# Expert outputs of a decoder layer: gathered and summed at the end, or scattered with accumulation as each tile is done

## The chip, the cores and the metric

The kernel runs on one core of a Trainium2 chip. The metric is the device time of one execution in microseconds (us): the median of several runs. The core has five engines that work beside each other and meet at semaphores: PE (matrix products), DVE (vector operations), ACT (activations and copies), POOL (general, and the issue of indirect DMAs) and SP (issue of DMAs). ACT and POOL issue DMAs too. Each engine does its instructions in order.

## What is computed

x is 4 sequences of 1024 tokens of 256 numbers. The reference is a decoder layer of three blocks:

```python
# after a gated delta-rule attention block on x (L0_attn) and its layernorm:
x = _layernorm(x + _L0_xattn_ref(x, ctx_1024, _lenS2, ...), axis=-1)
x = _layernorm(x + _L0_ffn_ref(x, router_w, gate_w, gate_b, up_w, up_b, down_w, down_b), axis=-1)

# _L0_ffn_ref: 8 experts, each token uses 2
probs = jax.nn.softmax(xf @ router_w.T, axis=-1)
topv, topi = jax.lax.top_k(probs, TOP_K)
mask = jnp.zeros_like(probs).at[jnp.arange(n)[:, None], topi].set(1.0)
probs = probs * mask
probs = probs / (probs.sum(axis=-1, keepdims=True) + 1e-09)
g = jnp.einsum('nd,edf->nef', xf, gate_w) + gate_b
u = jnp.einsum('nd,edf->nef', xf, up_w) + up_b
h = jax.nn.silu(g) * u
expert_out = jnp.einsum('nef,efd->ned', h, down_w) + down_b
y = jnp.einsum('ne,ned->nd', probs, expert_out)
```

The change is in the last block, in what leads to it, and in a few lines at the kernel's start.

## The kernel before

All numbers are 32-bit. P is 128, B is 4 sequences, D is 256, NE is 8 experts, FF is 512. Tokens are worked on in NS = 8 slabs of 4 x 128.

The first half (project, prepare, scan and their helpers) is the delta-rule attention. It leaves its normalized result in the DRAM tensor xd. At the start of the program, lines 141 to 155 make the DRAM tensors xg and yg, turn the gate and up biases with one transpose into br, store them as rows in bd (L149, on SP) and fill the end of xg with zeros (L153, on ACT).

The cross-attention is a software pipeline over 64 units (slab, sequence, half of the heads): five stages with fixed distances (L1165), interleaved with the generator route of the slab before. Slabs are in SBUF tiles xs with three buffers (slab_in). Route computes a slab's softmax over the experts, its two best experts as one-hot rows sel, their shares, and for both a row of xg: expert e owns a stretch of STRIDE rows, and counts in free say how far it is filled. Then POOL scatters the slab's rows twice, 8 indirect DMAs of 128 rows each (L1145). Shares and rows of all slabs are kept in share and at. For slabs 0 to 4 the slab is stored back to xd and its buffer loads slab i + 3.

When the last unit is done, the memory of the attention is released; SP loads the down weights wdn (L1179), and copies gate, up and down biases to all partitions of ball by two broadcasting DMAs (L1184 and L1188: 4 MB and 1 MB written). ACT reads eight numbers into registers one after another and writes 128 rows of zeros behind each expert's last row (L1264). The function tiles computes from the counts which expert and which rows of xg each of the NT = 71 tiles of 128 rows has (ei, ri), and, with gap and moved, where each token's two results will lie in yg (found).

The loop over tiles (L1337) has five steps at fixed distances: fetch (a DMA of 128 rows of xg into mx, four buffers, three tiles ahead; the first four from ACT, the rest from SP), turned (two transposes and a copy to mxT), hidden (gate and up products against the expert's weights, addressed by a register; DVE adds the biases as sge and pup, ACT does silu, DVE multiplies to mh), turn_h (four transposes and a copy to mhT) and down (the product pdn, DVE adds the bias as my, SP stores 128 rows of yg).

At the end, combine goes over the 8 slabs: for each of 4 sequences and 2 experts POOL gathers 128 rows of yg into part (L1352), DVE multiplies by the share and adds to the slab (L1358), then come mean and variance (L1362, L1363), square root on ACT (L1366), reciprocal and offset on DVE, normalization on ACT (L1370, four per slab) and the store. Slabs 5 to 7 are still in SBUF, the others are loaded again from xd.

Instructions are not in the order of the text: a scheduler puts each engine's instructions in order when the program is built, keeps the dependences, and gives each DMA one of eight semaphores per kind, so that an issue also waits for the earlier DMA of its semaphore.

## Time and profile before

| what | value |
|---|---|
| time, median of 3 runs | 1990.59 us (1987.02 to 1990.92) |
| profiled execution | 1989.58 us |
| its span on the core | 1987.8 us |
| PE busy | 1640.0 us, 83% |
| DVE busy | 1119.5 us, 56% |
| ACT busy | 918.3 us, 46% |
| POOL busy | 549.5 us, 28% |
| DMA moved | 98.97 MB, mean 50 GB/s |

The span is what the instructions of the profiled execution cover; its own time, as measured, is 1.8 us more. Busy times are sums over the whole span, and the stages have different limits, so they are read by stage. A name such as "pdn<-wdn,mhT" is the tile written and the tiles read; L1326 is a line of the kernel before; PEclk is the share of full speed that PE's clock was granted. Each 128-row fp32 product shows as two PE records. "Chain of waits" is the chain of work that ended last, followed back from the end.

### The profile page before, as it was taken

Reading aid. Unit: us, or ns where it says so; the run is one execution under the profiler, and the core shown is the slowest. Engines: PE = TensorE matmul, PEld = TensorE weight load, DVE = VectorE, ACT = ScalarE, POOL = GpSimd, SP = SyncE. Lnnn points to the kernel's source line nnn. Section 1 sums busy time; section 2 is a strip of 40 time slices with the busy share of each in tenths; the row PEclk is TensorE's granted clock in tenths of the full one; section 3 lists DMA queues with packets and bytes.
Section 4 is the critical chain, followed back from the end, with each engine's and each line's share of the span. In section 5 each row is a group of like instructions: output and inputs, shape, how many; then the busy total and the mean of one; then the engine's idle time right before and its main releaser. Section 6 shows DMA issues by size and latency. Waiting matters only on the chain.

```text
span 1987.8 us, 27920 instructions
## 1 busy us (share of the span) xinstructions
PE 1640.0 (83%) x9524; PEld 1163.7 (59%) x9524; DVE 1119.5 (56%) x3199; ACT 918.3 (46%) x2161; POOL 549.5 (28%) x503
## 2 busy tenths in 40 slices
PE   4678898979898888878899999999739999999900
PEld 2456575747575666744676777767616666666600
DVE  4748584857576767434466666566534444444444
ACT  3435463636464545332687776766412222222212
POOL 2222222131222222132345545555410000000065
PEclk9879898989898999789999999999869999999955
DMA  3011010110101011030401100100162111111144
GB/s 113 17 32 23 20 35 17 28 27 22 32 22 33 22 22 44 17 113 0 169 12 33 42 23 32 43 33 22 33 239 77 46 46 46 48 43 48 32 147 136
DMA packets 118347, 98.97 MB, mean 50 GB/s; under 512 B 57803, under 2 KB 106303, under 8 KB 117951
## 3 DMA queue, kind: packets, MB, share of 16 engines
q1 hardware_dynamic: 107135, 75.66, 13.0%
q0 software_dynamic: 6144, 16.79, 2.7%
q10 hardware_dynamic: 4928, 4.74, 0.7%
q8 instruction: 78, 1.28, 0.3%
q14 instruction: 62, 0.51, 0.1%
HBM read 62.12 MB, written 35.03 MB: 49 GB/s over the span
## 4 chain that ended last, share of the span: by engine, by line
PE 49%; DVE 22%; ACT 11%; POOL 8%; issue 5%; DMA 5%; SPq 0%; ACTq 0%; POOLq 0%; DVEq 0%
PE pgt L1299 6%; PE pup L1299 6%; PE pdn L1326 6%; ACT sc L1006 4%; PE pp L257 3%; DMA part<-yg,found 2%; DVE kq L269 2%; DVE v L269 2%; PE pe L432 2%; PE pxo L1040 2%; PE pss L365 2%; DVE bp L455 2%; DVE ut L494 2%; PE pmh L1317 2%; POOL xg L1145 2%
## 5 line engine op out<-in xcount | busy, mean ns | idle before, releaser
L1006 ACT ACTIVATE sc<-sc,ntop,rq 128x77 f32<-128x77 f32 x512 | 182.2, 440 | 71.0 <-DVE ntop L1004 48.2
L1352 POOL DMA_INDIRECT part<-yg,found x64 | 61.3, 958 | 454.7 <-issue 443.7
L1040 PE MATMUL pxo<-vo,aT 128*128 128x256 f32 (+1 forms) x640 | 168.4, 396 | 3.7 <-ACT aT L1025 2.8
L1308 ACT ACTIVATE sge<-sge 128x512 f32<-128x512 f32 x71 | 44.7, 630 | 247.8 <-DVE sge L1307 247.8
L257 PE MATMUL pp<-nT,wqkv 128*128 128x262 f32 x512 | 143.3, 413 | 0.0
L1299 PE MATMUL pgt<-wall,mxT 128*128 x284 | 135.5, 600 | 1.8 <-ACT mxT L1288 1.8
L1299 PE MATMUL pup<-wall,mxT 128*128 x284 | 134.8, 597 | 0.0
L1326 PE MATMUL pdn<-wdn,mhT 128*128 x568 | 134.2, 379 | 0.0
L1040 PEld LDWEIGHTS pxo<-vo,aT 128*128 128x128 f32 (+1 forms) x640 | 117.9, 199 | 21.5 <-ACT aT L1025 5.8
L963 POOL TENSOR_TENSOR rq<-rq,nhalf 128x8 f32<-128x8 f32 x64 | 106.0, 1656 | 76.1 <-DVE rq L962 73.5
L949 PE MATMUL pq<-xwq,xT 128*128 128x512 f32 x256 | 123.0, 603 | 0.5 <-ACT xT L943 0.5
L1011 POOL TENSOR_TENSOR sc<-sc,den 128x616 f32<-128x616 f32 x64 | 77.9, 1218 | 160.7 <-DVE den L1010 77.6
L269 DVE SCALAR_TENSOR_TENSOR v<-pp,cols,v 128x256 f32<-128x256 f32 x192 | 91.3, 476 | 43.9 <-ACT v L267 42.0
L269 DVE SCALAR_TENSOR_TENSOR kq<-pp,cols,kq 128x256 f32<-128x256 f32 x192 | 90.5, 478 | 45.3 <-ACT kq L267 42.8
L257 PEld LDWEIGHTS pp<-nT,wqkv 128*128 128x128 f32 x512 | 96.1, 201 | 33.2 <-issue 16.8
L989 PE MATMUL psc<-kbd,qT 128*128 128x154 f32 x512 | 93.0, 305 | 27.1 <-DVE sc L996 21.9
L1307 DVE TENSOR_TENSOR sge<-pgt,ball 128x512 f32<-128x512 f32 x71 | 49.1, 692 | 112.9 <-PE pgt L1299 112.9
L1326 PEld LDWEIGHTS pdn<-wdn,mhT 128*128 128x128 f32 x568 | 102.5, 190 | 11.0
L685 POOL TENSOR_TENSOR so<-so,nhalf 128x4 f32<-128x4 f32 x32 | 32.4, 1011 | 276.0 <-DVE so L684 276.0
L989 PEld LDWEIGHTS psc<-kbd,qT 128*128 128x128 f32 x512 | 74.6, 196 | 43.3 <-DVE sc L996 30.1
L1299 PEld LDWEIGHTS pup<-wall,mxT 128*128 128x128 f32 x284 | 54.6, 192 | 69.0 <-issue 69.0
L455 DVE SCALAR_TENSOR_TENSOR bp<-pk,nb,ee 128x256 f32<-128x256 f32 x128 | 51.7, 476 | 69.9 <-PE pk L444 40.0
(285 smaller groups left out, 3700.8 us busy)
## 6 DMA issues: line engine op xcount, KB each, us to landing
yg<-my SPq DMA_DIRECT2D x71, 128.0 KB, 1.7
mx<-xg SPq DMA_DIRECT2D x67, 128.0 KB, 2.0
xs<-xd SPq DMA_DIRECT2D x13, 512.0 KB, 4.5
xi<-in_x SPq DMA_DIRECT2D x8, 512.0 KB, 4.1
am<-ab SPq DMA_DIRECT2D x16, 256.0 KB, 4.0
xd<-kd SPq DMA_DIRECT2D x32, 128.0 KB, 2.4
wall<-in_L_ffn_gate_w SPq DMA_DIRECT2D x8, 512.0 KB, 10.5
wall<-in_L_ffn_up_w SPq DMA_DIRECT2D x8, 512.0 KB, 10.8
```

What stands on the lines that cost most here:

```text
L257: mm(pp[:, 0 : 2 * (HALO + P)], lhsT=wqkv[:, kc, c * P : (c + 1) * P], rhs=nT[:, kc, 2 * j : 2 * j + 2, :].rearrange("p b t -> p (b t)"), ...
L269: nc.vector.scalar_tensor_tensor(ch, pre[:, :, n : n + P], cols[:, w0 + n : w0 + n + 1], ch, ALU.mult, ALU.add)
L455: nc.vector.scalar_tensor_tensor(bp[:, :, b * H + h], pk[:, r * 2 * P : (r + 1) * 2 * P].rearrange("p (n t) -> p n t", n=2), made["nb"][:, ...
L949: mm(pq, lhsT=t["xT"][:, kc, :], rhs=xwq[:, kc, c0 : c0 + HH * XD], start=kc == 0, stop=kc == KC - 1,)
L963: nc.gpsimd.tensor_tensor(rq, rq, nhalf[:, :HH], ALU.pow)
L989: mm(ps[:, c * 2 * SC : (c + 1) * 2 * SC], lhsT=qT[:, 2 * g + c, :], rhs=kbd[:, half * XC // 2 + 2 * g + c, b, :], start=True, stop=True,)
L1006: nc.scalar.activation(sc[:, h], sc[:, h], AF.Exp, scale=rq[:, h : h + 1], bias=ntop[:, h : h + 1])
L1011: nc.gpsimd.tensor_tensor(sc, sc, bc(den.unsqueeze(2), [P, HH, SC]), ALU.mult)
L1040: mm(px[:, 0:D], lhsT=aT[:w, c, :], rhs=vo[:w, b, half * NV + c, :], start=half == 0 and c == 0, stop=half == 1 and c == NV - 1,)
L1299: mm(ps, lhsT=t["xT"][:, c, :], rhs=wall[:, bass.ds(e * EW + off + c * FF, FF)], start=c == 0, stop=c == KC - 1,)
L1326: mm(px[:, 0:D], lhsT=t["hT"][:, f, :], rhs=wdn[:, bass.ds(e * EV + f * D, D)], start=f == 0, stop=f == FC - 1,)
L1352: nc.gpsimd.indirect_dma_start(out=g, out_offset=None, in_=yg, in_offset=bass.IndirectOffsetOnAxis(ap=found[:, i, b, k : k + 1], axis=0),)
```

## The change

- The row of a token in xg becomes DX = 260 numbers wide: behind its 256 values are the token's own row number in xd, the number of its first expert, and its two shares. Route writes these four columns into the slab tile xs (now 260 wide) before the scatter; share and at are no longer kept for all slabs, and found, gap and moved are gone. The zero rows behind the experts carry row numbers of 128 spare rows of xd.
- In down, four small DVE operations work out the weight of each row of the tile (mw: the first share where the tile's expert is the row's first expert, else the second) and its row number (mrow). ACT multiplies y by the weight, and POOL adds y to the rows of xd with an indirect DMA that accumulates. yg is gone. mx, mw and mrow have eight buffers, my four, mxT four. Fetch goes four tiles ahead and turned two.
- All eight slabs are stored back to xd after routing. combine loads every slab (five buffers), has no gathers, and the fourth of a slab's normalizations is done on POOL.
- ball is filled by PE: each bias row is copied to all partitions by a product with a column of the identity repeated 128 times, four rows to a PSUM bank, 20 banks, each copied to ball by ACT. The DRAM copy bd and both broadcasts are gone; the down biases come in as 16 rows (brd) at the start.
- The eight registers for the zero rows are loaded in one batch.

In the changed program's order, the banks' products are spread around pr and pcount of the last slab on PE, ACT does twelve of the 20 copies ahead of the load of the eight registers and the others between the zero fills, and each accumulating scatter on POOL waits for the one before. In the attention the engines' order is that of before but for a few places.

The core of the diff (not shown: the new constants, 0:D in place of whole slabs, and tex kept in another pool):

```diff
@@ -138,26 +142,28 @@
-    xg = tc.dram_tile([NROW, D], F32, name="xg")
-    yg = tc.dram_tile([NT * P, D], F32, name="yg")
-
-    bd = tc.dram_tile([2 * NE * FC, P], F32, name="bd")
+    xg = tc.dram_tile([NROW, DX], F32, name="xg")
+
     pbr = bank("pbr")
     nc.tensor.transpose(pbr[0 : 2 * NE * FC, 0:P], cols[:, C_GB:NCOLS], ident)
     br = const.tile([2 * NE * FC, P], F32, name="br")
     nc.vector.tensor_copy(br, pbr[0 : 2 * NE * FC, 0:P])
-    nc.sync.dma_start(out=bd, in_=br)
-    zero = const.tile([P, 1, D], F32, name="zero")
+    brd = const.tile([NE * KC, P], F32, name="brd")
+    nc.scalar.dma_start(out=brd, in_=a["L0_ffn_down_b"].rearrange("e (c n) -> (e c) n", n=P))
+
+    zero = const.tile([P, 1, DX], F32, name="zero")
     nc.gpsimd.memset(zero, 0.0)
+    nc.vector.tensor_scalar_add(zero[:, 0, D : D + 1], nw[:, N_PART : N_PART + 1], float(NS * B * P))
     nc.scalar.dma_start(
-        out=xg[NE * STRIDE :, :].rearrange("(p r) d -> p r d", p=P), in_=bc(zero, [P, NE, D])
+        out=xg[NE * STRIDE :, :].rearrange("(r p) d -> p r d", p=P), in_=bc(zero, [P, NE, DX])
     )
     ab = tc.dram_tile([2 * NQ * B * H, Q * Q], F32, name="ab")
     ub = tc.dram_tile([2 * NQ * B * H, Q * Q], F32, name="ub")
-    xd = tc.dram_tile([NS * B * P, D], F32, name="xd")
+    xd = tc.dram_tile([NS * B * P + P, D], F32, name="xd")
+    nc.scalar.dma_start(out=xd[NS * B * P :, :], in_=zero[:, 0, 0:D])
@@ -1046,13 +1052,11 @@
         if half == 1:
-            x = slabs[i][:, b, :]
+            x = slabs[i][:, b, 0:D]
             nc.vector.tensor_tensor(x, x, px[:, 0:D], ALU.add)
             layernorm(xp, x, x, "c")
-    slots, found = (ek.tile([P, NS, B, 2], I32, name=n) for n in ("slots", "found"))
-    at = ek.tile([P, NS, B, 2], F32, name="at")
-    share = ek.tile([P, NS, B, 2], F32, name="share")
+    slots = ek.tile([P, NS, B, 2], I32, name="slots")
@@ -1122,11 +1126,19 @@
         nc.vector.tensor_tensor(got, pair, bc(pw.unsqueeze(2), [P, B, 2, NE]), ALU.mult)
-        nc.vector.tensor_reduce(share[:, i], got, AX.X, ALU.add)
-        nc.vector.tensor_reduce(red, share[:, i], AX.X, ALU.add)
+        share = rp.tile([P, B, 2], F32, tag="share", name="share")
+        nc.vector.tensor_reduce(share, got, AX.X, ALU.add)
+        nc.vector.tensor_reduce(red, share, AX.X, ALU.add)
         nc.vector.tensor_scalar_add(red, red, 1e-9)
         nc.vector.reciprocal(red, red)
-        nc.vector.tensor_tensor(share[:, i], share[:, i], bc(red.unsqueeze(2), [P, B, 2]), ALU.mult)
+        nc.vector.tensor_tensor(xs[:, :, D + 2 :], share, bc(red.unsqueeze(2), [P, B, 2]), ALU.mult)
+        nc.vector.tensor_scalar(
+            xs[:, :, D], nw[:, N_STEP : N_STEP + B], nw[:, N_PART : N_PART + 1], float(i * B * P), ALU.add, ALU.add
+        )
+        first = rp.tile([P, B, NE], F32, tag="first", name="first")
+        number = nw[:, N_NUM : N_NUM + NE].unsqueeze(1)
+        nc.vector.tensor_tensor(first, sel[:, 0], bc(number, [P, B, NE]), ALU.mult)
+        nc.vector.tensor_reduce(xs[:, :, D + 1], first, AX.X, ALU.add)
         yield
@@ -1137,8 +1149,9 @@
         nc.vector.tensor_tensor(got, pair, bc(place.unsqueeze(2), [P, B, 2, NE]), ALU.mult)
-        nc.vector.tensor_reduce(at[:, i], got, AX.X, ALU.add)
-        nc.vector.tensor_copy(slots[:, i], at[:, i])
+        at = rp.tile([P, B, 2], F32, tag="at", name="at")
+        nc.vector.tensor_reduce(at, got, AX.X, ALU.add)
+        nc.vector.tensor_copy(slots[:, i], at)
         for b in range(B):
@@ -1149,8 +1162,8 @@
                 apart(ins, "scatter")
+        nc.sync.dma_start(out=tokens(i), in_=xs[:, :, 0:D])
         if i + 3 < NS:
-            nc.sync.dma_start(out=tokens(i), in_=xs)
             slabs.append(slab_in(sp, i + 3))
@@ -1181,16 +1194,21 @@
     ball = bl.tile([P, B_D + NE * D], F32, name="ball")
-    nc.sync.dma_start(
-        out=ball[:, 0:B_D].rearrange("p (n c) -> p n c", c=P),
-        in_=bc(bd.rearrange("(o n) c -> o n c", o=1), [P, 2 * NE * FC, P]),
-    )
-    nc.sync.dma_start(
-        out=ball[:, B_D:],
-        in_=bc(a["L0_ffn_down_b"].rearrange("(o e) d -> o (e d)", o=1), [P, NE * D]),
-    )
     for _ in routing:
         pass
+
+    for src, n, off in ((br, 2 * NE * FC, B_G), (brd, NE * KC, B_D)):
+        for r in range(0, n, 4):
+            pb = bank("pball", "sp", 3)
+            for q in range(4):
+                mm(
+                    pb[:, q * P : (q + 1) * P],
+                    lhsT=bc(ident[0:n, r + q : r + q + 1], [n, P]),
+                    rhs=src,
+                    start=True,
+                    stop=True,
+                )
+            nc.scalar.copy(ball[:, off + r * P : off + (r + 4) * P], pb)
     x_scope.close()
@@ -1237,32 +1255,18 @@
         nc.vector.tensor_copy(ri, row)
-
-        n = NS * B * 2
-        flat = at.rearrange("p i b k -> p (i b k)")
-        gap = t("gap", [P, n, NE])
-        behind = nw[:, N_FREE : N_FREE + NE]
-        nc.vector.tensor_scalar(nt, nt, 1.0 * P, -1.0 * STRIDE, ALU.mult, ALU.add)
-        nc.vector.scalar_tensor_tensor(
-            gap, bc(flat.unsqueeze(2), [P, n, NE]), -1.0 * STRIDE, bc(behind.unsqueeze(1), [P, n, NE]), ALU.add, ALU.is_gt
-        )
-        nc.vector.tensor_tensor(gap, gap, bc(nt.unsqueeze(1), [P, n, NE]), ALU.mult)
-        moved = t("moved", [P, n])
-        nc.vector.tensor_reduce(moved, gap, AX.X, ALU.add)
-        nc.vector.tensor_tensor(flat, flat, moved, ALU.add)
-        nc.vector.tensor_copy(found, at)
-        return ei, ri
+        return ei, ri, ex_
     behind = ek.tile([P, NE], I32, name="behind")
     nc.vector.tensor_scalar_add(behind, free, 1.0)
-    for e in range(NE):
-        row = nc.values_load(
-            behind[0:1, e : e + 1], engines=(mybir.EngineType.Activation,), min_val=0, max_val=NROW - P,
-            skip_runtime_bounds_check_because="within the expert's rows and the tile behind them",
-        )
-        apart(nc.scalar.dma_start(out=xg[bass.ds(row, P), :], in_=zero[:, 0, :]), "scatter")
-    ei, ri = tiles()
+    _, ends = nc.values_load_multi_w_load_instructions(
+        behind[0:1, :], engines=(mybir.EngineType.Activation,), min_val=0, max_val=NROW - P,
+        skip_runtime_bounds_check_because="within the expert's rows and the tile behind them",
+    )
+    for end in ends:
+        apart(nc.scalar.dma_start(out=xg[bass.ds(end, P), :], in_=zero[:, 0, :]), "scatter")
+    ei, ri, ex_ = tiles()
     r_scope.close()
@@ -1276,7 +1280,7 @@
         )
-        t["x"] = ep.tile([P, D], F32, tag="mx", name="mx", bufs=4)
+        t["x"] = ep.tile([P, DX], F32, tag="mx", name="mx", bufs=8)
         (nc.scalar if j < 4 else nc.sync).dma_start(out=t["x"], in_=xg[bass.ds(t["row"], P), :])
@@ -1284,7 +1288,7 @@
             nc.tensor.transpose(pt[:, c * P : (c + 1) * P], t["x"][:, c * P : (c + 1) * P], ident)
-        t["xT"] = ep.tile([P, KC, P], F32, tag="mxT", name="mxT", bufs=3)
+        t["xT"] = ep.tile([P, KC, P], F32, tag="mxT", name="mxT", bufs=4)
         nc.scalar.copy(t["xT"].rearrange("p c n -> p (c n)"), pt[:, 0 : KC * P])
@@ -1330,12 +1334,31 @@
             )
-        y = ep.tile([P, D], F32, tag="my", name="my", bufs=3)
+
+        e0, w = t["x"][:, D + 1 : D + 2], ep.tile([P, 2], F32, tag="mw", name="mw", bufs=8)
+        mine = ex_[:, j : j + 1]
+        nc.vector.scalar_tensor_tensor(
+            w[:, 0:1], e0, mine, t["x"][:, D + 2 : D + 3], ALU.is_equal, ALU.mult
+        )
+        nc.vector.scalar_tensor_tensor(
+            w[:, 1:2], e0, mine, t["x"][:, D + 3 : D + 4], ALU.not_equal, ALU.mult
+        )
+        nc.vector.tensor_tensor(w[:, 0:1], w[:, 0:1], w[:, 1:2], ALU.add)
+        row = ep.tile([P, 1], I32, tag="mrow", name="mrow", bufs=8)
+        nc.vector.tensor_copy(row, t["x"][:, D : D + 1])
+        y = ep.tile([P, D], F32, tag="my", name="my", bufs=4)
         nc.vector.tensor_tensor(y, px[:, 0:D], ball[:, bass.ds(e * D + B_D, D)], ALU.add)
-        nc.sync.dma_start(out=yg[j * P : (j + 1) * P, :], in_=y)
-
-    for j in range(-3, NT + 3):
-        for step, ahead in ((fetch, 3), (hidden, 0), (turn_h, -1), (turned, 1), (down, -2)):
+        nc.scalar.activation(y, y, AF.Identity, scale=w[:, 0:1])
+        nc.gpsimd.indirect_dma_start(
+            out=xd,
+            out_offset=bass.IndirectOffsetOnAxis(ap=row, axis=0),
+            in_=y,
+            in_offset=None,
+            compute_op=ALU.add,
+        )
+
+    for j in range(-4, NT + 3):
+        for step, ahead in ((fetch, 4), (hidden, 0), (turn_h, -1), (turned, 2), (down, -2)):
             if 0 <= j + ahead < NT:
@@ -1343,21 +1366,11 @@
     def combine(i):
-        xs = slab_in(ep, i) if i + 3 < NS else slabs[i]
+        xs = ep.tile([P, B, D], F32, tag="xs", name="xs", bufs=5)
+        nc.sync.dma_start(out=xs, in_=tokens(i))
         mv = ep.tile([P, B, 2], F32, tag="mv", name="mv")
         for b in range(B):
             x = xs[:, b, :]
-            for k in range(2):
-                g = ep.tile([P, D], F32, tag="part", name="part", bufs=8)
-                nc.gpsimd.indirect_dma_start(
-                    out=g,
-                    out_offset=None,
-                    in_=yg,
-                    in_offset=bass.IndirectOffsetOnAxis(ap=found[:, i, b, k : k + 1], axis=0),
-                )
-                nc.vector.scalar_tensor_tensor(
-                    x, g, share[:, i, b, k : k + 1], x, ALU.mult, ALU.add
-                )
             st = ep.tile([P, 6], F32, tag="st", name="st", bufs=4)
@@ -1367,6 +1380,11 @@
         for b in range(B):
+            if b == 3:
+                nc.gpsimd.tensor_scalar(
+                    xs[:, b, :], xs[:, b, :], r[:, b : b + 1], nm[:, b : b + 1], ALU.mult, ALU.add
+                )
+                continue
             nc.scalar.activation(
                 xs[:, b, :], xs[:, b, :], AF.Identity, scale=r[:, b : b + 1], bias=nm[:, b : b + 1]
             )
```

More of the change, by code (lines that the diff above doesn't have):

```diff
@@ L44 @@
 NROW = NE * STRIDE + NE * P
+DX = D + 4
 EW = 2 * KC * FF
@@ L66 @@
 N_LT = N_ROWS + 2 * H * 4
-N_FREE = N_LT + NE * NE
+N_NUM = N_LT + NE * NE
+N_FREE = N_NUM + NE
 N_STEP = N_FREE + NE
@@ L93, in _consts @@
     narrow[:, N_LT : N_LT + NE * NE] = (e[None, :] < e[:, None]).reshape(-1)
+    narrow[:, N_NUM : N_NUM + NE] = e
     narrow[:, N_FREE : N_FREE + NE] = e * STRIDE - 1
@@ L790, in slab_in @@
     def slab_in(pool, i):
-        xs = pool.tile([P, B, D], F32, tag="xs", name="xs", bufs=3)
-        nc.sync.dma_start(out=xs, in_=tokens(i))
+        xs = pool.tile([P, B, DX], F32, tag="xs", name="xs", bufs=3)
+        nc.sync.dma_start(out=xs[:, :, 0:D], in_=tokens(i))
         return xs
@@ L937, in queries @@
         if t["half"] == 0:
-            x = slabs[t["i"]][:, t["b"], :]
+            x = slabs[t["i"]][:, t["b"], 0:D]
             pt = bank("pxt", "pt")
@@ L1227, in tiles @@
         )
-        ex_, row = t("tex", [P, NT]), t("trow", [P, NT])
+        ex_, row = ek.tile([P, NT], F32, name="tex"), t("trow", [P, NT])
         nc.vector.tensor_reduce(ex_, past, AX.X, ALU.add)
```

## Prediction

> **What bounds the kernel now.** I read the busy table by stage first: the cross-attention stage, the routing of the last slab, the start of the tiles, the expert tiles, the tail. Columns: the stretch, its length, busy time of PE, PE's weight loads, DVE, ACT and POOL (with instructions), PE's granted clock, DMA share, GB/s.
>
> ```profile
> core 0: us, PE busy (x) PEld busy (x) DVE busy (x) ACT busy (x) POOL busy (x), PEclk, DMA share, GB/s
> 1300.00:1437.00 137.00, 118.65 (x619) 92.15 (x617) 83.35 (x246) 88.27 (x235) 75.71 (x68) 0.95 0.08 27
> 1437.00:1449.00 12.00, 5.36 (x22) 4.77 (x22) 5.30 (x27) 1.30 (x3) 0.23 (x1) 0.50 0.92 290
> 1449.00:1474.00 25.00, 0.61 (x2) 0.29 (x2) 7.89 (x26) 0.00 (x0) 8.38 (x8) 0.50 0.96 349
> 1474.00:1500.00 26.00, 24.18 (x72) 12.99 (x72) 9.09 (x14) 7.13 (x13) 0.00 (x0) 0.87 0.10 31
> 1500.00:1893.00 393.00, 392.53 (x1490) 246.93 (x1488) 168.93 (x270) 101.42 (x202) 0.00 (x0) 1.00 0.16 49
> 1893.00:1988.00 95.00, 0.00 (x0) 0.00 (x0) 44.27 (x144) 18.96 (x40) 61.30 (x64) 0.52 0.48 145
> ```
>
> Three stages matter. The tiles (1500 to 1893) are PE's: 392.53 of 393 us. The pdn groups in the chain below repeat every 5.82 us, so 71 tiles are 413 us; DVE has 168.93/67.5 = 2.5 us of work per tile, ACT 1.5, POOL none. The tail (95 us) has no PE; POOL issues 64 gathers there. The 25 us before the first tile have PE idle and the DMA engines 0.96 busy.
>
> Then the chain of waits, for what ends each of these two gaps (start, length, engine, what):
>
> ```profile
> 1438.89 3.66 PE pr L1079 x16
> 1451.04 14.54 DMA xg<-zero
> 1466.48 1.93 DMA xg<-zero
> 1469.54 3.79 DMA mx<-xg
> 1474.67 3.75 PE pgt L1299 x4
> ...
> 1889.07 3.47 PE pdn L1326 x16
> 1903.49 2.77 DMA part<-yg,found
> 1908.51 2.72 DMA part<-yg,found
> ```
>
> The first tile waits for zero fills of 128 KB that land 14.54 us after issue. The issue table says why: the 4 MB broadcast of the biases is on the engines at that time. (Line, queue, count, KB each, median us to landing.)
>
> ```profile
> ball<-bd SPq DMA_DIRECT2D x1, 4096.0 KB, 14.3
> ...
> xg<-xs,slots POOLq DMA_INDIRECT x64, 2.4
> xg<-zero ACTq DMA_DIRECT2D x8, 128.0 KB, 14.3
> ball<-in_L_ffn_down_b SPq DMA_DIRECT2D x1, 1024.0 KB, 5.0
> part<-yg,found POOLq DMA_INDIRECT x64, 2.8
> ```
>
> In the tail a gather occupies POOL 0.95 us and the next starts 0.30 later: 64 x 1.25 = 80 us. That is POOL's issue rate, and the tail's bound.
>
> **The tail.** Removed: 64 gathers, 64 multiply-adds on DVE (484 ns each). Kept: per slab of 512 KB a load, four bn pairs on DVE (about 0.38 + 0.17 each, so 2.3 us), the square root (0.30 on ACT), two small DVE operations, the normalization (0.58 each on ACT, about 0.5 start to start; three now, the fourth moves to POOL, hidden beside them), the store. A slab's latency after its load is about 2.3 + 0.5 + 0.5 + 1.6 = 4.9 us.
> The last three tiles finish y at 1889.1, 1891.3 and 1893.0; their scatters run one after another. With the period of 4.0 us taken below, and 0.7 for ACT, they end at 1893.8, 1897.8 and 1901.8. Only then can SP load slabs: xs<-xd has a median of 4.5 us, so slab 0 is there at 1906.3 and the others follow about 1.6 us apart (512 KB at 320 GB/s, between the table's 290 and 349). DVE takes the first five at 2.3 us each, to 1917.8; store 4 issues at about 1920.4. There are five buffers, and SP's order in the changed program is five loads, stores 0 and 1, load 5, stores 2, 3 and 4, load 6, store 5, load 7, stores 6 and 7. Load 5 issues at about 1917 (store 0, 3.3 us after 1913.5), lands at 1921.5, and store 5 goes out at 1926.4; load 7 stands behind it on SP, lands at 1930.9, and store 7 goes out at 1935.8. Today the end is 3.7 us after the last store's issue, so 1939.5. The tail is 46.5 us instead of 94.8: **-48**. Bounds: 8 MB moved at 320 GB/s plus the 9 us of scatters and the last slab's 4.9 + 3.7 is 44 us, -51; loads that take twice 4.5 us at each of the three waits give -35.
>
> **The scatters in the loop.** Each of the 71 tiles gets an accumulating scatter of 128 KB on POOL. In POOL's order each waits for its predecessor's landing, so the period is issue to landing plus the next dispatch. No accumulating DMA is in this trace. From below: a plain scatter, 2.4 + 0.30 = 2.7 us. From above: the destination is first read like a whole gather (2.8), then written like a whole scatter: 2.8 + 2.4 + 0.30 = 5.5. I take 4.0, half way, since a DMA must do both but may overlap them. Both ends are under PE's 5.82, so the loop costs 0; the end costs only the last three, about 3 us of tail for each us of period (-4 to +5). The cover is thin at the upper end: 0.3 us.
> Here the Trainium skill speaks against the change: "DMA: Bandwidth & Descriptors", the rules for kernel authors, says that an accumulate reads its destination and writes it later, with nothing holding the bytes, so that an accumulate on the same bytes must wait for the earlier one's semaphore. That is the chain just described; four y buffers don't shorten it. The same page's fit for one POOL-issued DMA (anatomy of one DMA) is 2.0 us plus bytes/436e3: 2.3 us for 128 KB, an estimate that the row's 2.4 bears out, and 2.6 if the bytes count twice, so a period of 2.9 and a tail shorter by 3. I keep the rows' 4.0.
> Who is queued behind: on POOL nobody. But DVE's write of my waits for the scatter four tiles back, and mrow for the one eight back; behind them on DVE are sge, pup and mh of the next tile, and PE waits for mh. This bites only from a period over 5.82.
> Other additions per tile: four DVE operations of 128x1 (about 0.16 each, as the small routing rows), to 3.1 of 5.82 us; one scaling on ACT (0.58), to 2.1 of 5.82; both hidden under PE. yg's store on SP goes. Fetches go four tiles ahead instead of three, on SP alone now.
>
> **Routing to first tile.** Removed: 5 MB of broadcast; eight register loads become one batch; three 128x512 operations of 0.68 on DVE that lay beside the waits. Added: 80 matmuls and 20 copies. In PE's order three banks come before or among the last pr, five between pr and pcount, twelve after; in ACT's, twelve copies precede the fills' register load and eight stand between the fills.
> A bank is four real 128-column matmuls. pdn gives 1.73/8 = 0.216 us per record, two records per 256-column matmul, so 0.22 per 128 columns, 0.87 a bank at full clock and 1.73 at half. The stage's clock is 0.50. About five matmuls get in ahead of pr at half clock (+2), then some 22 before pcount need about 5 to 6 us beside DVE's 5.1 us of routing (+0 to +1). So pcount and the slots come 2 to 3 us later: slots at 1452, eight scatters 1.27 apart issue until 1462.5, the last lands at about 1464 with the broadcast gone. Meanwhile PE's twelve last banks (10.4 us from 1450.5) and ACT's copies (0.57) and fills (0.4) end at about 1461. The fetch goes at 1464.5, lands 2.0 later (the median of the loop's fetches), and PE starts at about 1467 instead of 1473.4: **-6** (+2 to -10; if ACT's interleaved fills come last instead, the gain is gone).
> The clock: "TensorE: Matmul & The Clock Gate", part 1, puts the step to full speed about 4 us into sustained work and the step back after an idle window of 3.4 us. In this trace half speed held from 1474.67 to about 1481, some 6.6 us. By the rule the 20 banks cost 19 us, by the trace 21; and by both PE is cold again after 1461 to 1467. I take the trace and no gain at the first tile.
>
> **Start of the kernel.** The store of bd (8.06 on SP, behind DVE's br) no longer stands ahead of two input loads, and the 1 MB fill of xg moves behind the first three weight loads on ACT; but it now waits for DVE's write of zero. -1 (-3 to +1). Routing's four extra DVE operations per slab, under 1 us of a 60 us slab in which DVE is 61% busy: 0 to +3 in all, taken as 0. Rows of 1040 bytes instead of 1024: 0.
>
> **Sum.** -48 - 6 - 1 = -55. The profiled execution is 1989.58 us (span 1987.8), 1 us below the median of 1990.59. So 1989.58 - 55 = about **1934 us**.
>
> **Rivals.**
> 1. *The scatters become the bound* (slower). If an accumulate needs more than 5.82 us from issue to the next issue, POOL sets the tile's period through my and mrow. The gain is spent at 5.82 + 55/71 = 6.6 us. At 7.5 us: 71 x 1.68 = 119, so about 2054. For it: no accumulate was ever seen here, and the upper bound leaves 0.3 us. Against it: the DMA engines are 0.16 busy in this stage and POOL has nothing else. Chance 0.13.
> 2. *The gain is only the tail's issue rate* : the fills, banks and copies use up the transition, a period of about 5.9 to 6.3, or loads slowed by stores. -20 to -38, about 1960. For it: load 6 and 7 do stand behind stores on SP. Chance 0.11.
> 3. *Cheap accumulate, tail bound by DMA rate*: -60, about 1928; it lies inside the main case's range, 1920 to 1950, chance of both 0.74.
> 4. *Nothing gained*: a period near 6.6, or two of the above at once: within 0.2% (what a measurement of this kernel can tell from no change). Chance 0.02.
> Faster by over 0.2%: 0.85; within: 0.02; slower: 0.13. The range 1918 to 1970 leaves out the slower case and the worst of rival 2.
>
> **What would show it.** Scatters of xd with landing under 5.5 us, and pdn still every 5.82 us; a tail under 50 us with no POOL chain; the first pmx near 1467; no wait of DVE my or mrow on a scatter. I am wrong if my's idle time is put down to the DMA of xd, if the tile's period grows, or if pr and pcount move by more than 5 us.

## The result, and the profile after

The changed kernel takes 2009.67 us (median of 4 runs, 2004.11 to 2012.62). The kernel before took 1990.76 us in the runs beside it. The ratio is 1.0092, 95% interval 1.0075 to 1.0109: about 18 us slower, where 1934 us was predicted. The profiled execution was the quickest of the four; its span is 2002.3 us, 14.5 more than that of before.

The stages of the changed kernel, with the same columns as the table of before: from the last normalised slab to the last count, to the first transpose of a tile, to the first result of a tile, the tiles, the tail.

```profile
core 0: us, PE busy (x) PEld busy (x) DVE busy (x) ACT busy (x) POOL busy (x), PEclk, DMA share, GB/s
...
1452.00:1471.00 19.00, 19.00 (x85) 17.73 (x83) 5.10 (x26) 6.02 (x12) 0.30 (x1) 0.50 0.81 256
1471.00:1496.00 25.00, 20.18 (x92) 19.60 (x92) 6.48 (x21) 6.89 (x12) 8.00 (x8) 0.50 0.29 99
1496.00:1515.00 19.00, 17.33 (x51) 9.10 (x52) 10.02 (x41) 6.00 (x11) 0.00 (x0) 0.80 0.27 74
1515.00:1956.00 441.00, 410.88 (x1513) 246.47 (x1511) 203.39 (x526) 130.33 (x273) 106.84 (x69) 1.00 0.25 39
1956.00:2002.00 46.00, 0.37 (x2) 0.00 (x0) 15.84 (x81) 16.28 (x34) 7.49 (x10) 0.56 0.65 191
```

The tail is down to 46 us from 95, as hoped. But the tiles take 441 us, in which PE is busy 410.88: it stands idle for 30 us of a stage in which it was busy for 392.53 of 393 (and 399 of 399 in the mended kernels below; the other 12 us lie inside PE's records, whose ends are modelled). And the attention ends late: its last slab is normalised at 1452.3, before at 1437.3.

The chain of waits in the middle of the tiles and at the end (start, length, what):

```profile
1757.42 3.77 DMA xd<-my,mrow
1761.19 0.02 issue
1761.21 0.08 DVE mrow L1348
...
1761.34 0.71 DVE pup L1313
...
1763.21 0.52 ACT my L1351
...
1763.99 3.80 DMA xd<-my,mrow
...
1954.27 3.83 DMA xd<-my,mrow
...
1958.83 3.64 DMA xd<-my,mrow
...
1963.20 3.79 DMA xd<-my,mrow
1967.01 3.93 DMA xs<-xd
```

Each tile's scatter is on the path: it lands, releases the cast of row numbers (the write of mrow), and only then do pup, mh and my of the tiles in work follow. From one scatter to the next it is 6.57 us. The last three, which follow one another with nothing between, are 4.4 to 4.6 us apart, well under PE's 5.82. So the scatter isn't too slow by itself; something waits for it that should not.

Which, the list of waits says (who waited for whom: us in total, times, longest):

```profile
DVE xs L1135 <- DMA xg<-xs,slots: 40.2, 5, 8.3
...
DVE mrow L1348 <- DMA xd<-my,mrow: 170.4, 63, 3.3
```

63 of 71 casts wait, 2.7 us each; of these 170 us only some 42 are lost, since DVE works 3.1 of the 5.82 us of a tile and has the rest to spare. The other line was not in the prediction at all: in the attention DVE stands still five times, 8 us each, ahead of L1135, the write of a token's row number into the slab.

One period of the loop, on DVE and POOL (start, length, engine, line, and in brackets the idle time ahead and what ended it):

```profile
1757.42 1.55 POOL L1352 DMA_INDIRECT xd<-my,mrow  x1 [5.08 <-ACT my L1351]
...
1757.69 0.69 DVE L1311 TENSOR_TENSOR sge<-pgt,ball 128x512 f32<-128x512 f32 x1
...
1761.21 0.15 DVE L1348 CAST mrow<-mx 128x1 int32<-128x1 f32 x1 [2.83 <-DMA xd<-my,mrow]
1761.34 0.70 DVE L1313 TENSOR_TENSOR pup<-pup,ball 128x512 f32<-128x512 f32 x1
```

The scatter that ends the wait at 1761.2 was issued at 1757.42: it is the newest, not the one eight tiles back. The listing of DVE's instructions shows how that can be. The row numbers come with the fetched rows, which run well ahead of the results, so nothing but the row-number buffer holds the cast back, and the scheduler puts the cast for tile n behind the result of tile n-8 and ahead of that of n-7 (in the trace, too: the casts counted, between the 15th and the 61st, stand so). With eight buffers the cast for tile n writes the one that the scatter of tile n-8 reads, and that scatter has only just been issued.

### The profile page after: what moved, and what is told of

The parts are those of the page before. It is cut to its first block, busy times and chain, and to the rows that moved or that the text cites. A ratio compares the mean times of both kernels' runs of the same rounds, so it can differ in the third digit from the quotient of the medians.

```text
span 2002.3 us, 28505 instructions
## 1 busy us (share of the span) xinstructions
PE 1684.1 (84%) x9684; PEld 1192.3 (60%) x9684; DVE 1123.9 (56%) x3438; ACT 953.6 (48%) x2244; POOL 601.9 (30%) x518
## 5 line engine op out<-in xcount | busy, mean ns | idle before, releaser
L1352 POOL DMA_INDIRECT xd<-my,mrow x71 | 109.9, 1548 | 371.5 <-ACT my L1351 362.7
L1351 ACT ACTIVATE my<-my,mw 128x256 f32<-128x256 f32 x71 | 36.1, 508 | 211.6 <-DVE my L1350 211.6
L995 PE MATMUL psc<-kbd,qT 128*128 128x154 f32 x512 | 96.9, 312 | 44.4 <-DVE sc L1002 39.3
L1348 DVE CAST mrow<-mx 128x1 int32<-128x1 f32 x71 | 10.9, 153 | 170.4 <-DMA xd<-my,mrow 170.4
## 6 DMA issues: line engine op xcount, KB each, us to landing
wall<-in_L_ffn_gate_w SPq DMA_DIRECT2D x8, 512.0 KB, 10.4
```

Source lines behind the costliest of these rows:

```text
L995: mm(ps[:, c * 2 * SC : (c + 1) * 2 * SC], lhsT=qT[:, 2 * g + c, :], rhs=kbd[:, half * XC // 2 + 2 * g + c, b, :], start=True, stop=True,)
L1351: nc.scalar.activation(y, y, AF.Identity, scale=w[:, 0:1])
L1352: nc.gpsimd.indirect_dma_start(out=xd, out_offset=bass.IndirectOffsetOnAxis(ap=row, axis=0), in_=y, in_offset=None, compute_op=ALU.add,)
```

## The experiments

All but the last were timed against the kernel before on the same chip (before: 1989.25 us beside the first four, 1990.83 beside the next four, 1995.1 beside the last two). "First to last result" is the time from the first to the last my; "slab to result" the time from the last normalised slab to the first my; the count is taken at the start of its last product, 0.6 to 0.7 us later than in the recorded expectations. In the kernel before they are 399.3 and 56.0 us, in the changed one 441.2 and 62.9.

Theory W: two small instructions, placed early by the scheduler because their data is early, wait on DVE for the scatter issued last. Rivals: the scatter's own pace (S), or a wait that shrinks with more buffers (D); for the attention, that the waits were covered (A).

| kernel | time, us | ratio to before (95%) |
|---|---|---|
| changed | 2009.67 | 1.0092 (1.0075 to 1.0109) |
| 12 row-number buffers | 2003.53 | 1.0081 (1.0055 to 1.0108) |
| 13 row-number buffers | 1963.22 | 0.9880 (0.9854 to 0.9907) |
| number written late | 1985.45 | 0.9982 (0.9970 to 0.9994) |
| biases by DMA | 2002.41 | 1.0084 (1.0054 to 1.0115) |
| both waits gone | 1945.50 | 0.9761 (0.9741 to 0.9781) |
| both, biases by DMA | 1942.57 | 0.9761 (0.9740 to 0.9782) |
| before, biases by PE | 1991.79 | 1.0008 (0.9998 to 1.0019) |
| both, scatter without addition | 1943.55 | 0.9764 (0.9744 to 0.9784) |
| both, PE's biases last | 1938.93 | 0.9725 (0.9710 to 0.9739) |
| both, biases half and half | 1929.58 | 0.9684 (0.9664 to 0.9703) |

### Twelve and thirteen buffers

The second run has bufs=13 in the same place.

```diff
-        row = ep.tile([P, 1], I32, tag="mrow", name="mrow", bufs=8)
+        row = ep.tile([P, 1], I32, tag="mrow", name="mrow", bufs=12)
```

> The changed kernel with twelve buffers for a tile's row numbers (mrow) instead of eight. Theory W (the cast of row numbers stands on VectorE so early that it waits for the scatter issued last, not for one eight back): in the listing of VectorE's instructions the cast for tile n still comes right behind the result of tile n-12, so twelve buffers buy nothing: period 6.6 us, time 2010, within 4. Rival S (the accumulating scatter itself, its 1.55 us on GpSimd and 3.8 us to landing, is the pace of the loop): also 2010. Rival D (distance counts: a wait for an older scatter the more buffers there are): half as many buffers again take most of the wait away, 1970 to 1985.

> One buffer more than in the run with twelve: thirteen for the row numbers. Theory W: the cast for tile n now needs the scatter of tile n-13, which is one tile period (5.8 us) older than the newest, more than its 3.8 us to landing; the 170 us of waits of the row casts fall below 10, the tile period goes back to 5.82 us, and the 41.9 us that the stretch from first to last result of a tile grew by (399.3 to 441.2) come back: 1968, between 1963 and 1974. Rival S: nothing changes, 2010. Rival D: 1970 to 1985, and the run with twelve is about as fast.

Measured: 2003.5 and 1963.2. The first is a little under the 2006 to 2014 expected, but its ratio can't be told from the changed kernel's; the second is at the lower end of theory W's range. With twelve the list of waits is as before,

```profile
DVE mrow L1348 <- DMA xd<-my,mrow: 159.3, 59, 3.5
```

and with thirteen the view of the row numbers shows who still waits for a scatter (last two lines), and the stage of the tiles is PE's again:

```profile
L1352 POOL DMA_INDIRECT xd<-my,mrow x71: 1535/1547/1607, 1517.5 to 1922.2; - x71
...
who waited for it (us, times):
  POOL xd L1352: 6.0, 2
  ACT sge L1312: 1.9, 1
```

```profile
1516.00:1915.00 399.00, 399.00 (x1513) 250.94 (x1512) 212.06 (x522) 136.77 (x273) 106.85 (x69) 1.00 0.28 43
```

First to last result falls from 438.0 us (twelve) to 399.1 (thirteen), to what it was before the change. The scatter still takes 1.547 us on POOL and its 3.8 to landing: rival S is out. Four more buffers gained 3 us of the 42 and one more gave the rest: rival D is out. In both traces the cast for tile n stands between the result of tile n-12 and that of n-11. With twelve buffers it needs the scatter of n-12, the newest; with thirteen one that is a whole tile older, and it runs directly behind the result without waiting:

```profile
1702.40 0.42 DVE L1350 TENSOR_TENSOR my<-pdn,ball 128x256 f32<-128x256 f32 x1 [0.89 <-PE pdn L1330]
1702.88 0.15 DVE L1348 CAST mrow<-mx 128x1 int32<-128x1 f32 x1
```

### The number written late

```diff
+        base = rp.tile([P, B], F32, tag="base", name="base")
+        nc.vector.tensor_scalar(base, red, 0.0, float(i * B * P), ALU.mult, ALU.add)
-        nc.vector.tensor_scalar(
-            xs[:, :, D], nw[:, N_STEP : N_STEP + B], nw[:, N_PART : N_PART + 1], float(i * B * P), ALU.add, ALU.add
-        )
+        nc.vector.scalar_tensor_tensor(
+            xs[:, :, D], nw[:, N_STEP : N_STEP + B], nw[:, N_PART : N_PART + 1], base, ALU.add, ALU.add
+        )
```

> The changed kernel with the row number of a token written into its slab only after the routing shares are there (through a small tile that depends on them; one VectorE operation of 4 numbers more per slab); eight row-number buffers as in the change. Theory W: in the changed kernel that write stands at the head of each slab on VectorE and waits 40.2 us in five places for the eight row scatters of the slab that had the buffer before; late, it waits for nothing, and the attention ends earlier by all of the 15.1 us that its end (last normalised slab, 1437.3 to 1452.3) moved: 1994, between 1990 and 2000. Rival A (the attention's end moved because the routing has four more VectorE operations a slab and the last slabs' row scatters stand ahead of the last normalisations on GpSimd): the waits of 40 us were covered, 2006 to 2010.

Measured: 1985.5; by the ratios 22 us less than the changed kernel, where theory W had about 15; the time lies below its range. The wait for the row scatters is gone from the list. The normalisations of the slabs (count, shortest/median/longest in ns, first to last start) in the changed kernel and here:

```profile
L187 DVE TENSOR_SCALAR xs<-xs,mvc,rsc x32: 411/413/471, 996.3 to 1452.3; 128x256 f32<-128x256 f32 x32
```

```profile
L187 DVE TENSOR_SCALAR xs<-xs,mvc,rsc x32: 411/412/415, 997.7 to 1435.2; 128x256 f32<-128x256 f32 x32
```

The attention is 437.5 us long instead of 456.0; before the change it was 436.6. So its growth was this wait, as closely as this stage repeats between executions (see the last experiments): rival A is out. Of the 40.2 us waited some 19 were on the path. I expected 15 because I read the end of the stage, 1437.3 to 1452.3, and forgot that it also began 4.4 us earlier. The operation reads only constants, so it was placed where the slab's buffer comes free, that is behind the eight row scatters of the slab that had the buffer before. One more small DVE operation per slab, which ties it to the shares, costs nothing that shows.

### The biases

The two broadcast DMAs are put back for PE's products, with bd, and all else is left as changed.

```diff
-    for src, n, off in ((br, 2 * NE * FC, B_G), (brd, NE * KC, B_D)):
-    ...
+    nc.sync.dma_start(out=ball[:, 0:B_D].rearrange("p (n c) -> p n c", c=P),
+        in_=bc(bd.rearrange("(o n) c -> o n c", o=1), [P, 2 * NE * FC, P]))
+    nc.sync.dma_start(out=ball[:, B_D:],
+        in_=bc(a["L0_ffn_down_b"].rearrange("(o e) d -> o (e d)", o=1), [P, NE * D]))
```

> The changed kernel with the biases brought to all partitions by the two broadcast DMAs of the kernel before instead of TensorE's 80 products and ScalarE's 20 copies; all else as changed. Theory B (TensorE's products at half clock stand between the router's product and the count, and ScalarE's copies between its zero fills of the tiles' ends): the stretch from the last normalised slab to the count goes from 18.4 back to 10.3 us, and that from the count to the first fetch from 22.8 to 14 to 18, because the table's chain got shorter and the fills no longer wait: 1996, between 1993 and 2003. Rival C (the first fetch waits for the row scatters and their landing, 8 us of GpSimd, whoever brings the biases): 2002 to 2006, only the part before the count. Rival Z (the broadcasts' 91% share of the DMA engines costs the weights what TensorE's time saved): 2006 to 2012.

Measured: 2002.4, where the ranges of theory B and rival C overlap; the ratio can't be told from the changed kernel's. From the last slab to the count it takes 11.0 us instead of 19.1, as theory B had it. But from the count to the first fetch it takes 22.8 us, no less than the changed kernel's 22.0. The issue table of this stretch shows what is late (KB each where it is given, median us to landing; the trace has the landing of only one of the eight in each row), and the row of the stretch why:

```profile
xg<-zero ACTq DMA_DIRECT2D x8, 130.0 KB, 14.5
...
xg<-xs,slots POOLq DMA_INDIRECT x8, 11.6
```

```profile
1463.00:1486.00 23.00, 0.50 (x3) 0.36 (x2) 6.47 (x21) 0.00 (x0) 8.00 (x8) 0.50 1.01 351
```

In the changed kernel the fills land in 2.0 us and the last slab's row scatters in 2.4 to 3.1. Here the last row scatter, issued at 1474.0, lands at 1485.6, and the first fetch goes out at 1485.9. So rival C fits this kernel in its reason too; that the last fill, whose landing the trace lacks, comes just as late is not excluded. It does not hold "whoever brings the biases". With the broadcasts fills and row scatters go out without delay and land late, on DMA engines that are full (a share of 1.01); with PE's products they land soon, but the fills go out late, each behind a copy on ACT that waits for its bank:

```profile
1461.08 9.75 PE L1204 MATMUL pball<-br,sq 64*128 64x128 f32 x44
...
1470.76 0.65 PE L1124 MATMUL pcount<-ahead,sq 128*128 128x40 f32 x2
...
1483.99 7.19 PE L1204 MATMUL pball<-brd,sq 16*128 16x128 f32 x32
...
1489.51 0.58 ACT L1211 COPY ball<-pball 128x512 f32<-128x512 f32 x1 [1.12 <-DMA xg<-zero]
1489.65 0.34 ACTq L1268 DMA_DIRECT2D xg<-zero  x1
1491.22 0.58 ACT L1211 COPY ball<-pball 128x512 f32<-128x512 f32 x1 [1.12 <-DMA xg<-zero]
1491.36 0.34 ACTq L1268 DMA_DIRECT2D xg<-zero  x1
```

The count waits out 22 products (44 records) of 9.75 us although DVE's work for it was done by 1466.3. The last fill goes out at 1491.4 and lands as the first fetch starts, 2.1 us later. (The brackets name a fill as what ended ACT's wait; but the copies come 1.71 us apart, which is PE's time for a bank, and the last starts at 1491.22, right after PE's last product at 1491.18.)

The same exchange alone, in the kernel before:

> The kernel before with TensorE's bias products and ScalarE's copies in place of its two broadcast DMAs, nothing else of the change. Theory B: the stretch from the last normalised slab to the count grows by 8 us, from 10.3 to 18 to 19; from there to the first fetch it stays at 22 to 24, now held by the fills behind ScalarE's copies instead of by full DMA engines; first fetch to first result a little shorter: 5 to 7 us slower than before, 1994 to 1997. Rival (the broadcasts' bytes gone from the busiest stretch of the DMA engines is a gain once the routing is not delayed otherwise): 1980 to 1989.

Measured: 1991.8, ratio 1.0008 (0.9998 to 1.0019), 1.6 us where 5 to 7 were expected. The stage grew somewhat more than expected: slab to result is 63.8 us, 7.8 more, and the first fetch comes 42.5 us after the slab instead of 31.3. In this profile what offsets it is the start: the first normalised slab comes at 994.5 instead of 1000.7, while attention, tiles and tail (94.8 us, 95.2 before) are as they were. The unchanged kernel's second profile (the last run below) has it at 996.9, so most of this can be spread between two executions; why the median of twelve runs grew by so little is open.

### Both waits gone, with either way for the biases

These join the mends above: thirteen buffers and the number written late; the second also has the broadcasts. The edits are those shown above.

> The changed kernel with both mends that went singly before: thirteen buffers for row numbers, and the row number written late into the slab. Theory W: the two waits lie in different stages, so their gains add, 44 and 22 us off the changed kernel's 2008 on the same chip: 1942, between 1937 and 1947, a ratio of 0.974 to 0.979 to the kernel before. Rival (one shift hides the other, since the first tile is then held by TensorE's bias products and not by the attention's end): 1947 to 1958.

> The same with the biases brought by the two broadcast DMAs. Theory B as it stands after the first runs (DMA biases give back 8 us before the count, but the first fetch then waits for their 5 MB on the DMA engines, so that only 5 us are left): 1937, between 1932 and 1942. Rival: with the attention's end earlier the weights are still in flight, so that the broadcasts collide more and the two ways are equal, 1940 to 1946.

Measured: 1945.5 and 1942.6, ratio 0.9761 for both. The first lies in its range: the two gains add, as theory W had it for waits in different stages. The two ways for the biases can't be told apart here (slab to result 62.4 and 59.3 us), which was the rival's case for the second kernel; 1937 had been expected. The second kernel's trace also shows that it is the broadcast that delays: of its fills, the four that went out ahead of it (1450.9) landed in 2.0 to 3.6 us, those behind it, where the trace has the landing, in 14.9 to 16.4; the last fill landed at 1468.4, the last row scatter at 1468.1, and the first fetch went out at 1468.7.

### The scatter without its addition

```diff
             in_offset=None,
-            compute_op=ALU.add,
```

> The kernel with both waits gone, its result scatters without the accumulation: the addition to the residual stream is left out, the rows are overwritten. It prices the accumulation. Theory W (a scatter's length is off the path while nothing waits for the newest one): the tile period stays at 5.82 us; issue on GpSimd falls from 1.55 to about 1.0 us and landing from 3.8 to 2.5 us, of which only the last scatter's share counts: 1 to 3 us faster than the kernel with both waits gone. Rival S (the accumulation costs the loop's row fetches and stores DMA time): 6 us or more faster.

Measured: 1943.6, 2 us under the kernel with both waits gone (1 to 3 expected), and the intervals of the two ratios overlap. (This kernel leaves out the sum: each row of xd keeps only what was written last.) The view of the scatter, on POOL and to landing:

```profile
L1354 POOL DMA_INDIRECT xd<-my,mrow x71: 957/962/971, 1500.4 to 1902.3; - x71
...
DMA to landing us min/median/max: 2.4/2.4/3.1
```

So the addition costs 0.6 us of POOL's time and 1.4 us of landing per tile, and with nothing waiting for it the loop doesn't feel either: 399.1 us from first to last result. Behind the last result the tail is 41.4 us instead of 45.1.

### Moving and sharing the biases

First, PE's bias loop moved in the program from ahead of x_scope.close() to behind ei, ri, ex_ = tiles(); then, at the same place, only the gates' 32 products by PE, up and down by broadcast DMAs:

```diff
     ei, ri, ex_ = tiles()
+    for src, n, off in ((br, 2 * NE * FC, B_G),):
+        for r in range(0, NE * FC, 4):
+            pb = bank("pball")
...
+    nc.sync.dma_start(out=ball[:, B_U:B_D].rearrange("p (n c) -> p n c", c=P),
+        in_=bc(bd[NE * FC :, :].rearrange("(o n) c -> o n c", o=1), [P, NE * FC, P]))
```

> The kernel with both waits gone and TensorE's biases, but their 80 products and 20 copies stand in the program behind the table of tiles instead of ahead of it. Theory F (TensorE's 34 us of bias products at half clock, 20 banks at 1.71 us, are a floor under the first tile wherever they stand): the last normalised slab to the count falls from 19.1 to 11 us, the fills go out at once, but the first tile's transposes come behind the last product, 11 + 34 = 45 us after the slab instead of 44.4: 1945, between 1941 and 1949. Rival G (what the products cost is the 8 us ahead of the count): 1934 to 1939.

> Both waits gone; the gates' biases by TensorE (32 products, 8 copies, behind the table of tiles), those of up and down by broadcast DMAs (3.1 MB instead of 5.2). Theory F and its counterpart for the DMA engines (at 0.3 MB a us the 2.1 MB left out are 7 us): the count comes 11 us after the last slab, TensorE's 8 banks take 14 us beside the row scatters, and the first fetch comes 16 to 18 us after the count instead of 22: 1937, between 1934 and 1941, below both kernels with one way for all biases (1943 and 1945). Rival: the weights, not the broadcasts, hold the fetch's landing, 1941 to 1946.

> The kernel before, unchanged, profiled once more, for the spread of a stage between two profiled executions. In the kernel before with TensorE's biases the stretch from the last normalised slab to the first result grew by 7.8 us and yet the time by 1.6 us; its scans and attention ended 6.6 us earlier in its profile. If that is spread, the attention here ends anywhere between 1430 and 1438 with the stretch behind it at 56.0 within 0.5; if it was an effect of the change, the attention ends at 1437 within 1.5.

Measured: 1938.9 for all on PE but last, 1929.6 for half and half; the unchanged kernel took 1989.72 in its one run. In the first, the count comes 11.0 us after the slab and the fills go out at once, and still the first transpose comes 46.7 us after the slab (44.4 with the products ahead), right behind the last product at 1474.8: theory F's floor. Slab to result is 63.9 us, 1.5 more than with the products ahead. Yet the time lies below theory F's range and in rival G's, whose reason the profile refutes. The gain is in the attention: 431.2 us, where the profile with the products ahead shows 440.2. The unchanged kernel has 436.6 in its first profile and 432.8 in its second, whose attention ended at 1429.7 with 56.2 us from slab to result (its tail took 102.8 us, so that its time is that of the first): such an early end is spread, not an effect of the exchange. The rows of the attention show what it goes with: the kernel before twice, both waits gone, the products last.

```profile
1000.70:1437.30 436.60, 396.94 (x2077) 305.57 (x2075) 278.18 (x814) 305.00 (x808) 235.72 (x202) 0.97 0.09 30
```

```profile
996.90:1429.70 432.80, 389.48 (x2077) 299.80 (x2075) 277.45 (x813) 305.02 (x808) 235.74 (x202) 0.99 0.09 30
```

```profile
999.80:1440.00 440.20, 402.08 (x2086) 309.76 (x2085) 273.36 (x841) 305.23 (x808) 235.61 (x203) 0.96 0.09 32
```

```profile
996.90:1428.10 431.20, 389.88 (x2077) 299.91 (x2075) 271.49 (x842) 304.87 (x808) 235.93 (x202) 0.99 0.10 33
```

The same work on PE takes 402 us at a granted clock of 0.96 and 390 at 0.99; what grants the one or the other to the same program is not shown. The time of one kernel follows the clock from run to run (the number written late: 1992.1 us at a mean clock of 0.916, 1978.3 at 0.929), so runs of equal mean clock compare better than medians. There are few: at 0.919 the kernel with the products ahead took 1945.2 us and this one 1943.9, at 0.925 1939.9 and 1938.6. By these, moving the products gained about 1 us, and most of the lead in the median is the clock.

Half and half, from the last slab on: to the count, to the first fetch, to the first result, the tiles:

```profile
1427.00:1438.00 11.00, 4.89 (x21) 4.43 (x21) 5.41 (x28) 1.30 (x3) 0.00 (x0) 0.50 0.91 296
1438.00:1457.00 19.00, 14.47 (x67) 14.07 (x66) 6.47 (x21) 4.30 (x8) 8.00 (x8) 0.50 0.95 334
1457.00:1478.00 21.00, 16.74 (x51) 8.85 (x52) 10.13 (x45) 6.01 (x11) 0.00 (x0) 0.78 0.37 108
1478.00:1877.00 399.00, 399.00 (x1513) 250.85 (x1511) 212.08 (x522) 136.76 (x273) 106.78 (x69) 1.00 0.27 43
```

PE's 14 us of products now lie beside the row scatters, behind the count, and the smaller broadcasts delay less: the fill of the issue table lands in 11.2 us instead of 14.5, the last row scatter in 7.9 instead of 11.6. The first fetch comes 19.2 us after the count (16 to 18 expected). Slab to result is 51.2 us, 8 to 13 less than with one way for all biases and 5 less than before. This kernel is 3.2% faster than the one before (0.9684, 0.9664 to 0.9703) and the fastest here. It came out 7 us under the 1937 expected, below the range; its attention, like that of the kernel with the products last, was short in the profile (430.8, at a clock of 0.99). At equal mean clock it took 1937.4 us against 1948.4 with all biases on PE (0.917) and 1929.6 against 1939.9 (0.925): these 10 to 11 us are what the stage got shorter.

## Why the prediction was wrong

Two of the signs of being wrong that it named came: the tile's period grew, to 6.57 us, and the count moved by more than 5. By its own steps, from the two profiled executions, whose spans differ by +14.5:

| step | predicted, us | measured, us |
|---|---|---|
| tail | -48 | -49.3 |
| scatters in the loop | 0 | +41.9 |
| routing's added operations | 0 (to +3) | +19.4 |
| start of the kernel | -1 | -4.4 |
| routing to first tile | -6 | +6.9 |
| sum | -55 | +14.5 |

- **The tail** was right in its mechanism and, with some luck, to 1 us. The sum lets load 5 wait for store 0 at 1913.5, where its own 4.9 us after the load at 1906.3 put that store at 1911.2, so it has the end over 2 us too late; against that the last scatter landed 10.6 us after the start of the last result (1956.4 to 1967.0), where it had 9.2. The period of the scatters was right too: 4.0 taken, 4.4 to 4.6 measured (3.8 to landing and 0.7 to the next issue), between the bounds 2.7 and 5.5. The fit of the Trainium skill ("DMA: Bandwidth & Descriptors", anatomy of one DMA) had given 2.6 us to landing with the bytes counted twice; the trace's 3.8 decides.
- **The loop is the step that failed: "so the loop costs 0".** It said that DVE's "write of my waits for the scatter four tiles back, and mrow for the one eight back", and that "this bites only from a period over 5.82". That takes eight buffers for a distance of eight tiles, as if the cast ran beside the result it belongs to. It runs eight results earlier, so the eight buffers buy no distance: the wait is for the newest scatter, and it bites though the scatters' own period, 4.4 to 4.6 us, is well under 5.82. 63 waits of 2.7 us became 42 us on the path; one buffer over the twelve tiles of run-ahead removed them. Rival 1 had the sign and the place (through mrow) but not the cause: the scatter never was the bound.
- **The attention** was the second failed step, in the same way: I costed the four added operations of routing by their length, under 1 us a slab, and not by what they wait for. One of them, the row number, waited 40.2 us. Written late, it waits no more, and the stage went from 456.0 to 437.5 us.
- **Routing to first tile** failed in its price for PE's products. The prediction had the 22 products before pcount at "about 5 to 6 us" and the twelve last banks at 10.4 us, which are the prices at full clock, though it had itself read 0.50 for the clock of this stage and worked out 1.73 us a bank for it. Its paragraph on the clock let the clock rise: 19 us for 20 banks by the rule it quoted, 21 by the 6.6 us of half speed that it read in the trace before (1474.67 to 1481 is 6.3). It did not rise, though PE had work all the time:

```profile
1452.00:1490.00 38.00, 38.00 (x171) 36.44 (x170) 11.59 (x47) 12.23 (x22) 8.31 (x9) 0.50 0.54 177
```

  The 22 products took 9.75 us, a bank 1.71, and the products behind the count 19.4 (1471.75 to 1491.18). With the products last in the program it was the same, and the tiles' products, which follow there without a gap, were at full clock about 7 us on:

```profile
1440.10:1474.80 34.70, 34.70 (x161) 34.25 (x161) 7.60 (x30) 10.65 (x19) 8.02 (x8) 0.50 0.40 125
```

```profile
1482.00:1484.00 2.00, 2.00 (x6) 0.88 (x6) 1.63 (x5) 0.37 (x1) 0.00 (x0) 1.00 0.24 71
```

  So neither the rule nor the rise in the trace before holds for these products, of 64 and 16 partitions and 128 columns; which of their properties does it is not shown. Of the 6.9 us, the count takes 8.2, count to fetch 1.6, and fetch to first result gives 2.9 back. The prediction's proviso, "if ACT's interleaved fills come last instead, the gain is gone", is what happened.
- **The start** came out 4.4 us earlier, but not clear of what the early stages differ between executions: the second profile of the unchanged kernel has its first normalised slab 3.8 us earlier than the first. Nor is the store of bd shown to be the cause: the three kernels that have it back begin at 995.0 to 996.2, the changed one at 996.3.

Not settled: why the exchange of the biases cost the kernel before only 1.6 us (at most 3.8), when its stage grew by 7.8; what sets PE's clock in the attention, with which it takes 431 to 440 us; and why the clock stays at half through PE's bias products.

## What to carry to other kernels

Where a scheduler places instructions, a buffer count is not a distance: find in the engine's listing how far ahead of its use an instruction stands, and give its output buffers for that run-ahead and for the time until its last reader is done (here twelve tiles and one more). Look above all at small operations that depend on early data or on constants alone; both that waited here had been placed where their buffer comes free, and held on DVE all that stood behind them; tie such an operation to something late or give it buffers. Price an operation at the clock that the stage shows. And before a difference of a few us is put down to an edit, compare the clock of the stages that the edit doesn't touch.

## What the runs showed of the hardware

- An accumulating indirect DMA of 128 rows of 1 KB takes POOL 1.55 us and lands in 3.8; the same without addition takes 0.96 and 2.4. Issued one behind the other's landing, the accumulating ones come every 4.4 to 4.6 us.
- The gates' biases on PE and the others by DMA was better than either way for all: with the 4 MB broadcast ahead of it a 130 KB fill took 14.5 us to land (14.9 to 16.4 in another kernel, whose fills ahead of the broadcast took 2.0 to 3.6) and the last row scatter 11.6; with 2 MB and the 1 MB of the down biases 11.2 and 7.9; with no broadcast 2.0 and 2.4 to 3.1. And 20 banks held PE for 34 us, eight for 14.
- PE's granted clock stayed at 0.50 through 38 us in which PE was busy all the time with small fp32 products (64 or 16 partitions by 128 columns, and the few of the routing), in the changed kernel, and for 34.7 us with the products last. The tiles' products brought it to 1.00 within about 7 us (1474.8 to 1482).
- In the attention the same program ran at a granted clock of 0.97 and of 0.99 in two executions, and PE's busy time was 396.9 and 389.5 us.
